# Two-layer graph attention on one core: the last three graphs' second attention is given other places in the table of steps

## The chip, the cores and the metric

The kernel runs on one core of a Trainium2 chip. TensorE (PE) multiplies, VectorE (DVE), ScalarE (ACT) and GpSimd (POOL) do the rest, and SyncE (SP) issues most DMA transfers. The metric is device time in microseconds (us), as the median of several runs. What a measurement of this kernel can tell from no change is taken to be 0.2%.

## The reference

Sixteen graphs of 1024 nodes with 256 features each go through two layers; all graphs share one adjacency matrix.

```python
h = relu(layernorm(x))
# layer 0: MLP, dense attention (no mask), MLP, attention masked by adj
out = relu(h @ mlp1_w + mlp1_b);  res = out
out = elu(gat(relu(out), None, W_fc, a_fc)) + res
out = relu(out @ mlp2_w + mlp2_b);  res = out
out = elu(gat(relu(out), adj, W_hand, a_hand)) + res
x = x + relu(out)
# layer 1: attention masked by adj
h = relu(layernorm(x))
x = x + relu(softmax(where(adj == 0, -1e9, leaky_relu(e_src + e_dst))) @ (h @ W))
```

In `gat`, h = inp @ W, the scores are leaky_relu(f1[i] + f2[j]), softmax runs over j, the weights multiply h, and the result goes through elu.

## The kernel before, in words

A graph is cut into eight tiles of 128 nodes (NT = 8); a half is four tiles, a pair is two (PAIR = 256 nodes). "a" names the first masked attention (layer 0, class Gnn0), "b" the second one (layer 1, class Gnn1). A suffix in a name of the profile is dropped: `ob` stands for the sums of the second attention of every graph.

The softmax weight of a masked attention factors. For a query row i and a node j it is max(row[i], w[j]) times the mask, with a factor d[j] that is put on the features beforehand. So a masked attention has these steps:

- `project` (L322, L324): features and the two score columns of a tile, TensorE `pa` or `pb`, copied by ScalarE to `hma` or `hmb`.
- `extremes` and `vectors` (L329 to L351): the largest score over all nodes by way of a small TensorE transpose (`extps`), then the exponentials `qwd`.
- `row` (L360 or L364): qwd's row on all partitions. Either it goes through DRAM and comes back by a DMA (`rowsa<-row_a`), or, for graph 0's and the last two graphs' steps, eight TensorE transposes write it to PSUM (`rowsps`) and ScalarE copies it in one piece (L364).
- `scale` (L368): ScalarE puts d[j] on the features of tile j, in place.
- `weight` (L373): VectorE makes 128 x 256 weights (`atta`, `attb`) for one pair of query tiles and one j. Eight buffers exist (ATT = 8), shared by a and b and by the dense attention of graph 0.
- `product` (L384): TensorE adds, for both tiles of the pair, the product with the features of tile j, into `oa` or `ob`. A matmul in float32 shows as two rows of the trace.
- `finish` (L396 to L400, L420 to L422): reciprocal on VectorE, Relu with this scale on ScalarE. For a, `combine` follows: two exponentials on ScalarE (L405, L406) and two adds on GpSimd (L408, L409); the adds are on VectorE for graph 0 alone. `update` adds to x on VectorE (L413 for a, L426 for b). `store` writes a half of x to DRAM from SP (L429).

The dense attention sorts nodes by score. GpSimd gathers rows of two tables of running sums from DRAM (`got`, L637, fine and coarse). `share` (L649 to L652, `den`) and `mean` (L659 on ScalarE, L661 on VectorE, `hp`) weigh them. `merge` transposes four `hp` for one of four feature chunks (L708, `hpT`), takes the minimum on VectorE (L710), two exponentials on ScalarE (L711, L712), and `merge_end` a maximum and sum on VectorE (L718) and an add on GpSimd to `resT` (L719). `mlp2` (L726) needs all four chunks of a half of `resT`; its result `oT` is projected to `pa`, and `natural` transposes it back (`on`, L740) to `o_nat` (L742 on ScalarE), which `combine` adds. `Norm` has `stats` (L262, L263 on VectorE), `root` (L267, L268 on GpSimd, a half at a time), `center` (L272 on VectorE, `hn`) and `turn` (L282 on TensorE, `nt`; L286 on ScalarE, `hT`).

PSUM has four buffers for matmul results (`mm`: project, products, MLPs), two for transposes (`tr`: extps, on, hpT, nt) and one for rows.

The order of the work is written by hand. `at(lo, hi, steps)` enters steps in a table at evenly spaced due times from lo on; the times are in about microseconds but are only used to sort. The sorted table is issued step by step, and each engine then runs its own instructions in exactly that order; a step waits only for data and for buffers. GpSimd's order is fixed in the same way. So a step that waits on an engine holds up all that stand behind it on that engine.

```python
    def base_of(b):
        return b * PERIOD - SHORT * (b > 0)      # PERIOD 142, SHORT 28
    ...
        for _, _, step in sorted(table, key=lambda entry: entry[:2]):
            ...
            step()
```

In the steady state a graph's second attention is done between the steps of the following graphs: its pair 0 before the next graph's first attention, its pairs 1 to 3 after that. Graph 13 (third from the end) still does so. Graph 14 does three pairs early, among the merges of graph 15, and the last pair after the first attention of graph 15. Graph 15 has nothing beside it. `dense_end` holds graph 15's share, mean and merges, which are set 10 later than for the others (`late`).

Of the kernel before, what the change touches and what calls it, by code (L numbers as in the profile page):

```python
# [31 lines left out]
def fast_path(ctx: ExitStack, tc: tile.TileContext, alarm, x, adj, w1, b1, w2, b2, w_fc, a_fc,  # L32
# [269 lines left out]
    class Masked:  # L302
# [53 lines left out]
        def row(self, sent=False):  # L356

            self.rows = work.tile([P, N], F32, tag="rows", name=f"rows{self.name}")
            if sent:
                nc.sync.dma_start(self.rows, row_d[self.which][self.b % 2].to_broadcast([P, N]))  # L360
            else:
                rows_ps = bc_psum(f"rowsps{self.name}")
                row_broadcast(rows_ps, cols(self.qwd[:, 0, :]))
                nc.scalar.copy(self.rows, rows_ps)  # L364
# [5 lines left out]
        def weight(self, q, j):  # L370

            a_t = big.tile([P, PAIR], F32, tag="att", name=f"att{self.name}_{q}_{j}", bufs=ATT)
            nc.vector.scalar_tensor_tensor(a_t, self.rows[:, q * PAIR:(q + 1) * PAIR],  # L373
                                           self.qwd[:, 1, j:j + 1],
                                           edge[:, j, q * PAIR:(q + 1) * PAIR], op0=OP.max,
                                           op1=OP.mult)
            self.att[q, j] = a_t

        def product(self, q, j):

            for t in (2 * q, 2 * q + 1):
                if j == 0:
                    self.out[t] = mm_psum(f"o{self.name}_{t}")
                nc.tensor.matmul(self.out[t][:, :F + self.ONES],  # L384
                                 lhsT=self.att[q, j][:, (t % 2) * P:(t % 2 + 1) * P],
                                 rhs=self.hm[:, j, 2:2 + F + self.ONES], start=(j == 0),
                                 stop=(j == NT - 1))

    class Gnn0(Masked):
# [13 lines left out]
        def combine(self, t, o_nat):  # L403
# [3 lines left out]
            adder = nc.vector if self.beside_gathers else nc.gpsimd  # L407
# [8 lines left out]
    class Gnn1(Masked):  # L416
# [11 lines left out]
        def store(self, h, xt, b):  # L428
            nc.sync.dma_start(out[b, h * HALF:(h + 1) * HALF, :].rearrange("(t p) f -> p t f", p=P),  # L429
                              xt[:, h * TH:(h + 1) * TH, :])  # L430
# [412 lines left out]
    def dense_end(t0, b):  # L843
        d = dense[b]
        late = 10 * last(b)
        for h in range(NH):
            lo = t0 + late + 78 + 13.4 * h
            at(lo, lo, [partial(d.share, h)])
            lo = t0 + late + 78.2 + 14 * h
            at(lo, lo + 1.5, each(d.mean, [h], range(TH)))  # L850
            merges(t0 + late + 85 + 13.2 * h, d, h)
        second_mlp(t0, b)
# [5 lines left out]
    def second_mlp(t0, b, after=0):  # L858
        d, m = dense[b], gnn0[b]
        for i, lo in enumerate((102.5, 104.8, 113, 116.5)):  # L860
            lo += t0 + 10 * last(b)
# [5 lines left out]
    def weights(m, q, lo, hi):  # L867
        at(lo, hi, each(m.weight, [q], range(NT)))

    def masked_first(t0, b):  # L870
# [10 lines left out]
        weights(m, 0, lo - 5.5, lo - 1)  # L881
        at(t0 + 10, t0 + 10, [partial(load_again, b)])
        at(t0 + 4.5, t0 + 11, each(dense[b].natural, range(NT // 2)))
        at(lo, lo + 28, each(m.product, range(NQ), range(NT)))
        for q in range(1, NQ):
            weights(m, q, lo - 5.5 + 7 * q, lo + 1 + 7 * q)
        for t in range(NT):
            end = lo + 7.2 + 7 * (t // 2) + 0.6 * (t % 2)
            at(end, end, [partial(m.finish, t)])
            at(end + 1.2, end + 1.2, [lambda t=t: m.combine(t, dense[b].o_nat)])  # L890
            at(end + 5.2, end + 5.2, [lambda t=t: m.update(t, xs[b])])
            end += 6.2 if last(b) or b == 0 else 9
            at(end, end, [partial(n.stats, t)])
        at(lo + 25, lo + 25, [partial(n.root, 0)])
        lo += 35.5 if last(b) or b == 0 else 38.5
# [5 lines left out]
    def second_norm(t0, b):  # L901
        n, m = norm2[b], gnn1[b]
        if last(b):
            n.turn_at(t0 + 46.5, 0)
            n.turn_at(t0 + 49, 1, 1.6)
            lo = t0 + 50
        elif b == 0:
            n.turn_at(t0 + 47, 0)
            n.turn_at(t0 + 50.5, 1, 1.6)
            lo = t0 + 47.2  # L910
        else:
# [5 lines left out]
        if last(b, 2):  # L917
            at(lo + 7.8, lo + 7.8, [m.vectors])
            at(lo + 8.2, lo + 8.2, [m.row])
            at(lo + 8.3, lo + 9.5, each(m.scale, range(NT)))  # L920
# [6 lines left out]
    def masked_second(parts, b):  # L927

        m = gnn1[b]
        for q, lo in enumerate(parts):  # L930
            at(lo, lo + 7, each(m.product, [q], range(NT)))
            weights(m, q, lo - 5.5, lo - 0.1)
            for u in range(2):
                t = 2 * q + u
                end = lo + 7.2 + 0.6 * u
                at(end, end, [partial(m.finish, t)])
                at(end + 1.5, end + 1.5, [lambda t=t: m.update(t, xs[b])])
            if q % 2:
                end = lo + 10
                at(end, end, [lambda h=q // 2: m.store(h, xs[b], b)])  # L940
# [79 lines left out]
    for b in range(NB):  # L1020
        base, after_base = base_of(b), base_of(b + 1)
        masked_first(base, b)
        second_norm(base, b)
        if last(b):
            parts = [base + 65 + 7 * q for q in range(NQ)]
        elif last(b, 2):
            parts = [base + 86, base + 94.5, base + 107.5, after_base + 39]
        else:
            parts = [after_base + lo for lo in (11, 46, 53, 60)]
# [21 lines left out]
    made, last = [], None  # L1051
    engine = mybir.EngineType
    with tc.manual_schedule(engines={engine.PE, engine.DVE, engine.Activation, engine.SP}):
        for _, _, step in sorted(table, key=lambda entry: entry[:2]):
# [4 lines left out]
            for ins in traced[n:]:  # L1059
                if ins.engine != engine.Pool:  # L1060
                    continue
                before = [] if last is None else [last]
                if is_scatter:
                    made.append(ins)
                else:
                    before, made, last = before + made, [], ins
# [446 lines left out]
```

## Time and profile before

| | us |
|---|---|
| median of 3 runs (2361.68 to 2363.62) | 2363.11 |
| the profiled execution, in all | 2353.15 |
| its span, first to last instruction | 2351.4 |
| TensorE busy in the span | 2271.9 |
| VectorE busy | 1620.2 |
| ScalarE busy | 1241.4 |
| GpSimd busy | 955.0 |

The prediction's sums are made against the span; what lies around it in that execution is 1.75 us. In the profile a group of instructions is named by line, engine and operation, and by the tile that it writes and those that it reads. PEclk is the share of TensorE's full clock that the throttle granted. A wait says which engine stood idle for which instruction of another engine, with the total, the number of times and the longest, in us. Idle time of an engine that doesn't set the end costs nothing.

### The profile page before, as it was taken

The numbers are of one execution on the slowest core, as the hardware profiler recorded it, in microseconds if no ns is written. First come the engines' busy times: TensorE is split into PE (matmuls) and PEld (weight loads), VectorE is DVE, ScalarE is ACT, GpSimd is POOL, SyncE is SP. The second block draws the span as 40 slices with busy tenths as digits, with TensorE's granted clock in tenths as the row PEclk, the third lists the DMA queues.
The fourth block names the chain that finished last, engine by engine and source line by source line (L and its number), as shares of the span: only waits on it lengthen the run. The fifth ranks groups of instructions, "written<-read, shape, count | busy, mean of one in ns | idle before, by whom it ended". The sixth has DMA issues, their size and how long they took to land. (4 is left out here: it accounts for less than half of the span.)

```text
span 2351.4 us, 30828 instructions
## 1 busy us (share of the span) xinstructions
PE 2271.9 (97%) x9955; PEld 1751.2 (74%) x9955; DVE 1620.2 (69%) x4499; ACT 1241.4 (53%) x2740; POOL 955.0 (41%) x1216
## 2 busy tenths in 40 slices
PE   8989999999999999999999999999999999999897
PEld 6667787777868777786876877777786877778676
DVE  6666685866858577685866767586685857758554
ACT  5345655647365554736556374564736556463442
POOL 1153435353433526444353533535344352634320
PEclk9999999999999999999999999999999999999898
DMA  4658366582646647275563645657265664637400
GB/s 175 166 160 208 72 178 163 168 199 102 196 117 171 179 158 189 90 192 145 180 180 133 176 109 177 160 169 192 105 194 118 175 179 152 186 101 199 109 1 29
DMA packets 150762, 355.81 MB, mean 151 GB/s; under 512 B 11112, under 2 KB 62648, under 8 KB 146496
## 3 DMA queue, kind: packets, MB, share of 16 engines
q1 hardware_dynamic: 103968, 189.58, 28.1%
q0 software_dynamic: 45952, 163.99, 26.3%
q8 instruction: 82, 1.34, 0.2%
q14 instruction: 88, 0.72, 0.1%
q10 hardware_dynamic: 672, 0.17, 0.0%
HBM read 227.40 MB, written 126.30 MB: 150 GB/s over the span
## 5 line engine op out<-in xcount | busy, mean ns | idle before, releaser
L384 PE MATMUL ob<-hmb,attb 128*128 128x257 f32 x2048 | 467.7, 386 | 11.8 <-DVE attb L373 11.6
L465 PE MATMUL h<-wfc_sb,resT 128*128 128x257 f32 x2048 | 465.5, 380 | 0.0
L384 PE MATMUL oa<-hma,atta 128*128 128x258 f32 x2048 | 455.5, 382 | 1.3 <-DVE atta L373 1.2
L384 PEld LDWEIGHTS ob<-hmb,attb 128*128 128x128 f32 x2048 | 388.9, 193 | 78.0 <-DVE attb L373 10.9
L384 PEld LDWEIGHTS oa<-hma,atta 128*128 128x128 f32 x2048 | 389.2, 190 | 60.2 <-issue 2.0
L465 PEld LDWEIGHTS h<-wfc_sb,resT 128*128 128x128 f32 x2048 | 379.5, 190 | 53.5 <-issue 0.7
L719 POOL TENSOR_TENSOR resT<-resT,e 128x512 f32<-128x512 f32 x128 | 163.4, 1276 | 374.3 <-DVE e L718 331.7
L408 POOL TENSOR_TENSOR posa<-posa,onat 128x256 f32<-128x256 f32 x120 | 100.5, 837 | 470.3 <-ACT posa L400 470.3
L373 DVE SCALAR_TENSOR_TENSOR atta<-rowsa,qwda,edge 128x256 f32<-128x256 f32 x512 | 267.3, 552 | 25.4 <-PE oa L384 14.3
L373 DVE SCALAR_TENSOR_TENSOR attb<-rowsb,qwdb,edge 128x256 f32<-128x256 f32 x512 | 243.6, 518 | 11.0 <-PE ob L384 8.4
L422 ACT ACTIVATE rb<-ob,recb 128x256 f32<-128x256 f32 x128 | 59.2, 476 | 341.5 <-DVE recb L420 338.5
L726 PE MATMUL m<-resT,w_sb 128*128 128x512 f32 x512 | 231.4, 598 | 4.4 <-POOL resT L719 4.4
L451 PE MATMUL m<-hT,w_sb 128*128 128x512 f32 x512 | 234.2, 596 | 0.5 <-ACT posa L400 0.5
L637 POOL DMA_INDIRECT got<-coarse,k x124 | 200.9, 1620 | 39.1 <-issue 35.1
L399 ACT ACTIVATE ea<-oa,reca 128x256 f32<-128x256 f32 x128 | 60.8, 475 | 265.3 <-DVE reca L396 265.3
L710 DVE TENSOR_SCALAR e<-hpT 128x512 f32<-128x512 f32 x128 | 88.4, 690 | 137.7 <-PE hpT L708 105.3
L726 PEld LDWEIGHTS m<-resT,w_sb 128*128 128x128 f32 x512 | 94.1, 192 | 107.0 <-issue 91.1
L451 PEld LDWEIGHTS m<-hT,w_sb 128*128 128x128 f32 x512 | 92.3, 192 | 95.3 <-issue 90.9
L637 POOL DMA_INDIRECT got<-fine,k x124 | 126.3, 1019 | 62.8 <-issue 33.4
L525 POOL DMA_INDIRECT sorted<-hnat,place x128 | 131.7, 1029 | 39.5 <-issue 18.9
L548 ACT ACTIVATE junk<-r,fs 128x1024 int8<-128x1024 f32 x124 | 142.4, 1148 | 6.5 <-POOL fs L469 5.5
L711 ACT ACTIVATE e<-e 128x512 f32<-128x512 f32 x128 | 80.7, 631 | 86.5 <-DVE e L710 86.4
(186 smaller groups left out, 3450.4 us busy)
## 6 DMA issues: line engine op xcount, KB each, us to landing
xs<-sorted SPq DMA_DIRECT2D x32, 1028.0 KB
fine<-tt SPq DMA_DIRECT2D x32, 1026.0 KB
fine<-xs SPq DMA_DIRECT2D x32, 1026.0 KB
x<-in_x_dram SPq DMA_DIRECT2D x16, 1024.0 KB
out_dram<-x SPq DMA_DIRECT2D x32, 512.0 KB
xn<-in_x_dram SPq DMA_DIRECT2D x15, 1024.0 KB
coarse<-carry SPq DMA_DIRECT2D x32, 256.5 KB
r<-row_r SPq DMA_DIRECT2D x14, 512.0 KB
```

Source lines behind the costliest of these rows:

```text
L373: nc.vector.scalar_tensor_tensor(a_t, self.rows[:, q * PAIR:(q + 1) * PAIR], self.qwd[:, 1, j:j + 1], edge[:, j, q * PAIR:(q + 1) * PAIR], ...
L384: nc.tensor.matmul(self.out[t][:, :F + self.ONES], lhsT=self.att[q, j][:, (t % 2) * P:(t % 2 + 1) * P], rhs=self.hm[:, j, 2:2 + F + self.O ...
L408: adder.tensor_add(pos, pos, o_nat[:, t, :])
L451: nc.tensor.matmul(ps, lhsT=w1_sb[:, kc, c * P:(c + 1) * P], rhs=hT[:, kc, h * HALF:(h + 1) * HALF], start=(kc == 0), stop=(kc == FC - 1))
L465: nc.tensor.matmul(ps[:, :F + 1], lhsT=self.resT[:, kc, t * P:(t + 1) * P], rhs=wfc_sb[:, kc, g, :], start=(kc == 0), stop=(kc == HC - 1))
L525: made = nc.gpsimd.indirect_dma_start(out=sorted_d[self.b % 2], out_offset=bass.IndirectOffsetOnAxis(ap=self.place[:, t:t + 1], axis=0), i ...
L548: nc.scalar.activation(junk, self.r2, AF.Sign, bias=self.fs[:, 0, t:t + 1], accum_out=self.signs[:, t:t + 1])
L637: nc.gpsimd.indirect_dma_start(out=got[u // n][:, u % n, :], out_offset=None, in_=(coarse_d if coarse else fine_d)[self.b % 2][:, :], in_o ...
L710: nc.vector.tensor_scalar_min(e, ps, 0.0)
L711: nc.scalar.activation(e, e, AF.Exp)
L719: nc.gpsimd.tensor_add(dst, dst, e)
L726: nc.tensor.matmul(ps, lhsT=w2_sb[:, kc, c * P:(c + 1) * P], rhs=self.resT[:, kc, h * HALF:(h + 1) * HALF], start=(kc == 0), stop=(kc == H ...
```

## The change

Only the places of steps, the size of a few pieces and one choice of engine change; the arithmetic is the same.

- `weight`, `product` and `store` take a first tile and a number of tiles instead of a pair or a half. Products of a part are entered in two groups, the last two j apart (`mid`).
- Graph 13: pair 0's weights are made 9.5 earlier; of pair 3, the last two j come 12.8 after the first six.
- Graph 14: parts are pairs 0 and 1, and then tiles 4, 5, 6, 7 alone. Pair 0 comes 8 earlier, pair 1 8.5 earlier, tile 4 9 earlier; tiles 5 and 6 come after graph 15's first attention, tile 7 after graph 15's second projection, its last two j behind the others. Each part is stored by itself.
- Graph 15: share, mean, merges and mlp2 come 13.4 earlier (`late` from +10 to -3.4). In both attentions the last pair is two single tiles. The adds of tiles 6 and 7 in its first attention go to VectorE as steps of their own (`add`), and norm steps move.
- Graphs 14 and 15: the four `natural` steps are spread between the steps of `vectors` and `row`. A row that comes from PSUM is copied in two pieces, 256 columns and 768; this holds for graph 0's first row too.

```diff
-                nc.scalar.copy(self.rows, rows_ps)
+                for i in (slice(0, PAIR), slice(PAIR, N)):
+                    nc.scalar.copy(self.rows[:, i], rows_ps[:, i])
...
-            adder = nc.vector if self.beside_gathers else nc.gpsimd
+            if not (last(self.b) and t >= NT - 2):
+                self.add(t, o_nat, nc.vector if self.beside_gathers else nc.gpsimd)
+
+        def add(self, t, o_nat, adder):
+            e, pos = self.out[t]
             adder.tensor_add(pos, pos, o_nat[:, t, :])
             adder.tensor_add(e, e, pos)
...
-        late = 10 * last(b)
+        late = -3.4 * last(b)
...
-            lo = t0 + late + 78.2 + 14 * h
-            at(lo, lo + 1.5, each(d.mean, [h], range(TH)))
+            lo = t0 + late + (78.2 + 14 * h if not last(b) else 80 + 12.2 * h)
+            at(lo, lo + 1.5 + 2 * last(b), each(d.mean, [h], range(TH)))
...
-            lo += t0 + 10 * last(b)
+            lo += t0 - 3.4 * last(b)
...
+        if last(b, 2):
+            for q, start in enumerate((0.5, 2, 4.2, 5.5)):
+                at(t0 + start, t0 + start, [partial(dense[b].natural, q)])
+        else:
+            at(t0 + 4.5, t0 + 11, each(dense[b].natural, range(NT // 2)))
+        pairs = [(t, 2) for t in range(0, NT, 2)]
+        if last(b):
+            pairs[-1:] = [(NT - 2, 1), (NT - 1, 1)]
...
+            if last(b) and t >= NT - 2:
+                at(end + 2.6, end + 2.6, [lambda t=t: m.add(t, dense[b].o_nat, nc.vector)])
+                end -= 2
...
-        at(lo + 25, lo + 25, [partial(n.root, 0)])
-        lo += 35.5 if last(b) or b == 0 else 38.5
+        at(lo + 25 - 3.4 * last(b), lo + 25 - 3.4 * last(b), [partial(n.root, 0)])
+        lo += 33.1 if last(b) else 35.5 if b == 0 else 38.5
...
-            at(lo + 7.8, lo + 7.8, [m.vectors])
-            at(lo + 8.2, lo + 8.2, [m.row])
-            at(lo + 8.3, lo + 9.5, each(m.scale, range(NT)))
+            at(lo + 7.1, lo + 7.1, [m.vectors])
+            at(lo + 9.2, lo + 9.2, [m.row])
+            at(lo + 9.3, lo + (10.5 if last(b) else 17), each(m.scale, range(NT)))
...
+        for lo, t, n, *apart in parts:
+            mid = apart[0] if apart else lo + 2.6 * n
+            at(lo, lo + 2.6 * n, each(m.product, [t], [n], range(NT - 2)))
+            at(mid, mid + 0.9 * n, each(m.product, [t], [n], range(NT - 2, NT)))
+            early = 5.5
+            if t == 0 and last(b, 3):
+                early = 2.6 if last(b, 2) else 15
+            weights(m, t, n, lo - early, lo - early + 5.4)
...
+            if last(b, 2):
+                at(end + 2.8, end + 2.8, [lambda t=t, n=n: m.store(t, n, xs[b], b)])
...
         if last(b):
-            parts = [base + 65 + 7 * q for q in range(NQ)]
+            parts = [(base + 65 + 3.5 * t, t, 2) for t in pairs[:-1]]
+            parts += [(base + 65 + 3.5 * t, t, 1) for t in (NT - 2, NT - 1)]
         elif last(b, 2):
-            parts = [base + 86, base + 94.5, base + 107.5, after_base + 39]
+            parts = [(base + 78, 0, 2), (base + 86, 2, 2), (base + 98.5, 4, 1),
+                     (after_base + 39, 5, 1), (after_base + 42.5, 6, 1),
+                     (after_base + 57.2, 7, 1, after_base + 59.3)]
         else:
-            parts = [after_base + lo for lo in (11, 46, 53, 60)]
+            parts = [(after_base + lo, t, 2) for lo, t in zip((11, 46, 53, 60), pairs)]
+            if last(b, 3):
+                parts[-1] = (after_base + 60.4, NT - 2, 2, after_base + 73.2)
```

## The prediction

> **What bounds the kernel now.** I read the page first.
>
> ```profile
> span 2351.4 us, 30828 instructions
> PE 2271.9 (97%) x9955; PEld 1751.2 (74%) x9955; DVE 1620.2 (69%) x4499; ACT 1241.4 (53%) x2740; POOL 955.0 (41%) x1216
> PEclk9999999999999999999999999999999999999898
> ```
>
> TensorE is busy 97% of the span at the full granted clock, until the last slices. The new program has the same 9128 TensorE instructions as the old in number, and the built order of every engine is the old one up to about 2105 us of this trace (only one ScalarE copy of graph 0 is cut in two). So only the last 245 us can move: the end of graph 13, and graphs 14 and 15. The table by stage says where they lose time (after the window: its length, PE, PEld, DVE, ACT and POOL busy, clock, DMA share, GB/s):
>
> ```profile
> 2110.00:2185.00 75.00, 71.36 (x333) 60.91 (x331) 57.29 (x149) 30.19 (x77) 35.87 (x36) 0.98 0.76 207
> 2185.00:2245.00 60.00, 48.60 (x176) 33.20 (x176) 32.58 (x75) 26.66 (x47) 12.21 (x12) 0.86 0.30 71
> 2245.00:2302.00 57.00, 49.99 (x229) 41.72 (x229) 35.16 (x93) 25.16 (x61) 15.40 (x21) 0.94 0.01 5
> 2302.00:2352.00 50.00, 39.11 (x169) 32.87 (x167) 20.51 (x61) 11.56 (x29) 0.00 (x0) 0.88 0.09 29
> ```
>
> Two losses stand here: idle TensorE (11.4 us in the second row) and a clock of 0.86 to 0.94. The waits of TensorE from 2100 us on name the first:
>
> ```profile
> PE ob L384 <- DVE attb L373: 5.5, 3, 2.1
> PE on L740 <- ACT onat L742: 2.9, 3, 1.2
> PE nt L282 <- ACT rb L422: 2.6, 1, 2.6
> PE hpT L708 <- DVE hp L661: 2.6, 3, 1.5
> PE m L726 <- POOL resT L719: 2.4, 2, 1.3
> PE rowspsb L238 <- ACT qwdb L347: 2.1, 2, 1.2
> ```
>
> With the smaller rows TensorE's gaps from 2110 us on add up to 25 us. The clock I followed in short windows. It is set in steps of 3.41 us, and a step runs at half rate when TensorE was little busy in the step before it:
>
> ```profile
> 2182.76:2186.17 3.41, 1.65 (x8) 0.96 (x6) 1.06 (x7) 0.85 (x4) 2.80 (x4) 1.00 1.06 224
> 2186.17:2189.58 3.41, 1.51 (x10) 1.28 (x11) 1.40 (x5) 2.63 (x7) 0.57 (x2) 1.00 1.06 226
> 2254.43:2257.84 3.41, 1.48 (x11) 1.14 (x11) 3.12 (x8) 3.41 (x9) 0.00 (x0) 1.00 0.01 2
> 2309.05:2312.46 3.41, 1.49 (x10) 1.09 (x10) 1.95 (x13) 1.38 (x5) 0.00 (x0) 1.00 0.02 5
> 2258.00:2259.00 1.00, 1.00 (x3) 0.78 (x3) 0.00 (x0) 1.00 (x3) 0.00 (x0) 0.50 0.00 0
> ```
>
> The steps after the second, third and fourth rows (busy 1.48 to 1.51 us) ran at 0.50; the one after the first (1.65 us) at full rate. Each half step full of work loses 1.7 us. After 2110 us about 13 us go this way.
>
> Here **a rule of the Trainium skill** differs: "TensorE: Matmul & The Clock Gate", section "Why this matters for your kernels", asks for no idle gaps over about 3 us. The longest gap here is 2.6 us, so by the rule no half step would arise and closing gaps would win the gaps alone. The trace shows half steps after several shorter gaps that add up to 1.9 us. I go by the trace. By the rule the clock's terms below drop out (1.7 at oa, 2.85 at ob 15, some 4.6 in the merges), and the sum would be 5.5 us instead of 14.6.
>
> **The change, stage by stage.** At full clock a matmul row of L384 takes 217 ns, an instruction (two such rows) 0.434 us, a tile's eight 3.47 us. Before: ob of graph 14 starts at 2189.2, pa of 15 at 2243.5, oa at 2257.6, pb at 2301.2, ob of 15 at 2313.6, the last matmul ends at 2344.4.
>
> *Up to ob of graph 14.* Transposes of o_nat now fill the gaps beside extpsa (L740's 2.9 us), and the first eight attb of graph 13 are made while VectorE idles 4.9 us before exta; their rows landed at 2086. But oa of graph 14 needs atta from rowsa, which lands at 2121.7 whatever TensorE does: it can start at about 2122.9 instead of 2124.0, gain 1. Next rstd waits for GpSimd's queue. Four products of ob 13 (1.74 us) now fill the wait before rowspsb; the gap after rowspsb (1.7 us) stays. New waits: recb of graph 13 stands behind the four den, and den needs the gathers' landing, at 2187 (the gathers' traffic falls at 2197 for the second half; the second store of graph 13, now later, frees about 1.6 us). On ScalarE the rows copy stands behind rb of that recb, and all eight scales of hmb behind it. Splitting the copy (1.01 us) lets attb start 0.6 us earlier, but hmb's first scale follows both pieces, so it brings nothing. ob 14 starts at 2188.9: gain 0.3 (between -1.5 and +3; nearest the low row, as the chain den, recb, rb, rows, hmb adds up to the 2.8 us that the filled wait and the earlier start win). Its half step I leave in (even chance).
>
> *ob 14 with the merges of graph 15, the largest term.* Before: 54.4 us. share, mean and merges move 13.4 us ahead in the table, and ob tile 5 goes out (3.47 us). Work: 40 x 0.434 + 8 transposed groups x 0.44 + 16 rows of m2 x 0.86 = 34.6 us. VectorE must deliver, from den to the last hp of the second half, 16 attb x 0.40 + 8 hp x 0.67 + 8 merge steps x 0.60 + den, recb and updates 3.5 = 20 us, plus about 2 us behind ScalarE's part and 2.5 us that a GpSimd add costs it. The last follows from these rows: beside GpSimd's adds the same instruction takes double.
>
> ```profile
> 2287.17 0.94 DVE L373 SCALAR_TENSOR_TENSOR attb<-rowsb,qwdb,edge 128x256 f32<-128x256 f32 x1
> 2288.37 0.47 DVE L373 SCALAR_TENSOR_TENSOR attb<-rowsb,qwdb,edge 128x256 f32<-128x256 f32 x1
> ```
>
> So the last hp comes at about 2212, where TensorE would need it at 2208: a wait of 3.8 instead of today's 6.1 (2.1+1.4+1.5+0.6+0.5). With 0.7+0.7 for two transposes, 1.9 before the last quarter of m2 (merge 0.7, ScalarE 0.63+0.72, merge 0.68, GpSimd 1.27 after its transpose, less 2.6 of m2 in between; today 2.35) and 3.2 for half steps: 34.6+3.8+1.4+1.9+3.2 = 45.0. Gain 54.4-3.5-45.0 = 6 (3 to 10).
>
> *pa to oa of graph 15.* From pa's end to oa 6.9 us now. After: on 0 fills the first gap, extps ends at +1.0, on 1 at +1.75, rowsps at +3.0, on 2 and 3 at +3.9; ScalarE's rows (0.4+0.8), onat (0.6) and first scale (0.5) end at +5.1. Gain 1.8, and no step stays under 1.6 us: 1.7 more. 3.5 (2 to 4).
>
> *oa 15 to pb 15.* Tiles 6 and 7 become single, their adds go to VectorE, root 0 moves ahead, ob 14's tiles 5 and 6 lie around the transposes. In VectorE's order the last atta of tile 7 stands behind four attb that wait for buffers of att (8) and four hn; it comes 0.7 to 2.2 us late. Behind it stand nine attb, three updates, three stats and two adds (6 us) ahead of tile 7's recb; then ScalarE 1.9, add, update and stats 1.4, GpSimd 1.4, hn 0.4 to 1.4. So pb follows oa's end by 12.5 us instead of 14.1, and oa ends 1.7+0.7 later than its work: about +0.5 loss (-3 to +3). The 128-wide instruction isn't in this trace; between nothing and the 0.40 of 256 columns I take 0.27, half the columns at the same start-up.
>
> *pb to ob 15.* Gaps 0.8, 0.9 and 1.6 and two half steps (2.85 us). Eight products of tile 7 (3.47 us) fill two of the gaps; after, 0.76+0.3+2.17+1.09+1.6 = 6.0 against 4.75 before plus 3.47 moved in: gain 2.2, and 2.85 of clock. Against it: x's last update of graph 14 stands ahead of the fourth attb and waits for rb, which stands behind eight scales on ScalarE (3.3 us): TensorE stops 1.5. Net 3.6 (2 to 5).
>
> *The end.* From the last matmul 7.0 us: reciprocal, Relu, update 1.2, a 512 KB store. Its packets take 2.4 us; 128 KB a quarter of it: gain 1.7 (1 to 2). SP's queue gets 11 stores for these two graphs instead of 4: behind graph 14's third stands x's load for 15, needed 30 us later, behind the others nothing. On GpSimd's queue only root 0 of graph 15 passes four adds, and a memset of hmb the last gather.
>
> Sum: 0.3+6+3.5-0.5+3.6+1.7 = 14.6; span 2351.4 to 2336.8. The profiled execution took 2353.15 in all; the median of the runs is 2363.11, 10 us above it. I carry the difference over: 2348.5.
>
> **Rivals.**
> 1. *All bubbles close*: VectorE keeps up, no half step but one. Left are some 8 us of gaps out of 25 and 2 of clock out of 13; the gain is 25 to 28, time 2337. For it: VectorE is 54% busy from 2185 to 2245. Against: the waits named are for VectorE.
> 2. *The bubbles only move*: a VectorE wait takes the place of each one closed in the merges and in oa's end; left are pa-oa 3.5 and the store 1.7 less 1 to 5: 2358 to 2363.
> 3. *Slower*: VectorE's queue bounds graph 15's first attention. From atta of tile 7 to hn of tile 7 stand about 50 instructions; if waits for att buffers and GpSimd's adds cost each 0.5 us on average, 25 us, it outweighs the rest: 2370. It decides from 0.4 us each. Against: only the adds of tiles 4 and 5 (3 us) run beside them.
> That the change doesn't do what it says is out: the built order shows it.
>
> **How the numbers follow.** Forecast 0.60, rival 1 0.18, rival 2 0.16, rival 3 0.06. Range 2337 to 2358. Bound of measurement 0.2% (4.7 us): faster 0.85 (forecast, rival 1, part of 2), same 0.10, slower 0.05. The forecast's own range is 2340 to 2356.
>
> **What would show it.** Until 2105 us the same trace. ob 14 at about 2189; pa 15 near 2234; TensorE's wait for hp under 4.5 us; waits for onat near 0; no half step at oa's start nor at ob 15's; a TensorE wait for atta near the end of oa 15, a gap of about 3 us before nt's second half; a stop of 1.5 us in ob 15's first pair; 5.3 us after the last matmul. Wrong if pa 15 isn't ahead of 2240, or the half steps stay in number.

## The result, and the profile after

The changed kernel takes 2356.33 us (median of 7 runs, 2351.53 to 2359.75), the kernel before beside it 2363.62 (7 runs, 2361.68 to 2366.51): a ratio of 0.9963, 95% interval 0.9951 to 0.9974. It is faster by some 7 to 9 us, where 14.6 were forecast. A second comparison (`after_again` below) gives 0.9961 (0.9948 to 0.9973): about 9 us. So the sign stands, and the size is half of the forecast or a little more. The median lies inside the whole range of 2337 to 2358, and 0.3 us above the range of the forecast case (2340 to 2356).

The page of the changed kernel, the lines that answer to those shown of before:

```profile
span 2357.9 us, 30868 instructions
PE 2268.6 (96%) x9955; PEld 1747.4 (74%) x9955; DVE 1625.7 (69%) x4535; ACT 1241.3 (53%) x2744; POOL 951.4 (40%) x1212
PEclk9999999999999999999999999999999999999999
```

The span of this execution is 6.5 us longer than the one of before (2351.4), though the kernel is faster. The order of instructions is the old one up to graph 14's `pa`, yet `pa` of graph 14 begins at 2116.5 us here and at 2103.1 before; in the profiles of the edits below it lies anywhere between 2096.5 and 2109.6. So the two profiles can't be compared by their spans. From `pa` of graph 14 to the end of the span they can: 248.3 us before, 241.4 after, 6.9 less.

The same windows as in the prediction, cut at the same distances from the same products (columns as there):

```profile
2123.42:2203.66 80.24, 71.31 (x329) 59.72 (x328) 54.53 (x142) 29.26 (x75) 36.52 (x38) 0.98 0.77 194
2203.66:2256.02 52.36, 43.36 (x165) 29.34 (x164) 31.79 (x76) 26.74 (x49) 11.72 (x11) 0.93 0.34 83
2256.02:2309.76 53.74, 47.09 (x231) 39.88 (x231) 37.98 (x116) 25.34 (x62) 12.43 (x17) 1.00 0.01 3
2309.76:2357.90 48.14, 39.31 (x183) 33.27 (x182) 23.51 (x78) 12.03 (x31) 0.00 (x0) 0.97 0.09 30
```

The last three stages are 60.0, 57.0 and 50.0 us before and 52.4, 53.7 and 48.1 now, and their clock rose from 0.86, 0.94 and 0.88 to 0.93, 1.00 and 0.97. The first stage went the other way, from 75.0 to 80.2. TensorE's waits from 2116 us on, longest groups first:

```profile
PE oa L385 <- DVE atta L375: 5.5, 3, 2.4
PE ob L385 <- DVE attb L375: 4.7, 2, 3.4
PE nt L282 <- DVE hn L272: 4.1, 2, 2.9
PE ob L385 <- ACT hmb L369: 3.7, 3, 2.1
PE hpT L713 <- DVE hp L666: 2.7, 4, 0.9
PE m L731 <- POOL resT L724: 2.2, 2, 1.1
...
PE on L745 <- ACT onat L747: 0.5, 2, 0.3
```

The wait for onat is nearly gone (2.9 before). That for hp is unchanged under this name (2.6), but of the 6.1 us of waits that the forecast counted there, the 2.1 for attb ahead of the merges are gone. New in the list are waits for atta, for hn and for the scaled hmb. TensorE's gaps above 0.15 us, from `pa` of graph 14 on, still add up to 26.7 us, 25 before, although 3.5 us of products were moved into them; 3.4 of the 26.7 are one wait behind a table that landed late in this execution (below). What fell is the clock's loss: ten steps at half rate (half steps) between 2105 us and the last product before, three now. Two of them with the steps ahead of them (windows as above):

```profile
2204.37:2207.78 3.41, 1.38 (x11) 1.03 (x9) 1.96 (x10) 1.94 (x6) 0.00 (x0) 1.00 1.06 208
2207.78:2211.19 3.41, 3.37 (x8) 2.72 (x9) 2.01 (x5) 3.41 (x8) 0.00 (x0) 0.50 1.06 209
2228.26:2231.68 3.42, 1.66 (x8) 0.87 (x8) 3.29 (x5) 1.23 (x2) 1.39 (x1) 1.00 0.00 0
2231.68:2235.09 3.41, 2.81 (x7) 1.94 (x7) 3.41 (x12) 2.07 (x4) 0.32 (x1) 0.50 0.00 0
```

1.38 and 1.66 us of TensorE work, and the next step at half rate: the wait for hmb at the start of ob 14, and the waits for hp.

Stage by stage, from the starts of the named tiles' products in the two traces (us; a gain is positive; 3.5 us of products moved from the second row to the fifth):

| stage | before | after | gain | forecast |
|---|---|---|---|---|
| pa to ob of graph 14 | 86.1 | 91.3 | -5.2 | 0.3 |
| ob of 14 to pa of 15, less the work moved | 54.4 | 46.7 | 4.2 | 6 |
| pa to oa of 15 | 14.1 | 12.3 | 1.8 | 1.8, and 1.7 of clock |
| oa to pb of 15 | 43.6 | 42.1 | 1.5, of which 1.7 clock | -0.5 |
| pb of 15 to the last product, with the work moved in | 43.2 | 42.3 | 4.4 | 3.6 |
| last product to the end | 7.1 | 6.7 | 0.3 | 1.7 |
| sum | 248.3 | 241.4 | 6.9 | 14.6 |

### The profile page after: what moved, and what is told of

The parts are those of the page before. It is cut to its first block, busy times and chain, and to the rows that moved or that the text cites. A ratio compares the mean times of both kernels' runs of the same rounds, so it can differ in the third digit from the quotient of the medians.

```text
span 2357.9 us, 30868 instructions
## 1 busy us (share of the span) xinstructions
PE 2268.6 (96%) x9955; PEld 1747.4 (74%) x9955; DVE 1625.7 (69%) x4535; ACT 1241.3 (53%) x2744; POOL 951.4 (40%) x1212
## 5 line engine op out<-in xcount | busy, mean ns | idle before, releaser
L375 DVE SCALAR_TENSOR_TENSOR atta<-rowsa,qwda,edge 128x256 f32<-128x256 f32 (+1 forms) x520 | 268.4, 545 | 27.6 <-PE oa L385 12.8
L375 DVE SCALAR_TENSOR_TENSOR attb<-rowsb,qwdb,edge 128x256 f32<-128x256 f32 (+1 forms) x536 | 247.9, 503 | 8.9 <-PE ob L385 5.5
L642 POOL DMA_INDIRECT got<-fine,k x124 | 125.7, 1013 | 74.4 <-DMA fine<-xs 41.9
```

The source lines that it names most:

```text
L375: nc.vector.scalar_tensor_tensor(a_t[:, :n * P], self.rows[:, i], self.qwd[:, 1, j:j + 1], edge[:, j, i], op0=OP.max, op1=OP.mult)
L642: nc.gpsimd.indirect_dma_start(out=got[u // n][:, u % n, :], out_offset=None, in_=(coarse_d if coarse else fine_d)[self.b % 2][:, :], in_o ...
```

## The experiments

Each kernel was compared with the kernel before on the same chip. Before takes 2351.2 us (median) beside the first four, 2350.0 beside the next four, 2356.2 beside the next three and 2350.7 beside the last; so ratios are compared, and 0.001 is 2.35 us. Theory at the start: the change works as forecast in graph 15's merges and attentions, and the 5.2 us lost ahead of `ob` of graph 14 are no work of it. Rivals: graph 13's part causes that loss; the bubbles only move.

**Graph 13's part undone** (`g13_back`)

```diff
-                early = 2.6 if last(b, 2) else 15
+                early = 2.6 if last(b, 2) else 5.5
...
-            if last(b, 3):
-                parts[-1] = (after_base + 60.4, NT - 2, 2, after_base + 73.2)
```

> The changed kernel with graph 13's part undone: its first attb again 5.5 us ahead of their products instead of 15, its last pair of ob again in one piece. In the changed kernel's profile the stage from pa to ob of graph 14 takes 91.3 us where it took 86.1 before (forecast 85.8). Theory: that loss is no work of the change; the table fine landed 3.5 us later in that one execution, GpSimd's gathers waited for it, and all behind them. Then this kernel's stage lies anywhere from 86 to 91 and its time is the changed kernel's or up to 2.8 us above it (four products no longer fill the wait before rowspsb, 1.7, and the start of oa, 1). Rival: graph 13's part causes the loss; then the stage is back at 86 in the profile and the time is 4 to 5 us below the changed kernel's, some 12 us below before.

Ratio 0.9948 (0.9935 to 0.9960); pa to ob of graph 14 takes 87.2 us. Neither theory is met in full: the stage isn't at 91, but without any edit it isn't at 91 in the other profiles either (below). Against three other profiles on this chip with graph 13's part in (87.7, 88.6 and 88.7) it is shorter by 0.4 to 1.5 us, and the ratio is lower by 0.0012 to 0.0015, within the intervals. So graph 13's part brings nothing that these runs show, and may cost 1 us (by the profiles) to 3 (by the ratios). In its profile the first row operation of graph 14 on VectorE after exta follows 0.3 us sooner: with the change two attb of graph 13 stand between exta and topa (at 7.8 to 8.7 us after pa), and not all eight in the idle time ahead of exta, as I had it.

**Merges and ob of graph 14 back** (`merges_back`)

```diff
-        late = -3.4 * last(b)
+        late = 10 * last(b)
...
-            parts = [(base + 78, 0, 2), (base + 86, 2, 2), (base + 98.5, 4, 1),
-                     (after_base + 39, 5, 1), (after_base + 42.5, 6, 1),
-                     (after_base + 57.2, 7, 1, after_base + 59.3)]
+            parts = [(base + 86, 0, 2), (base + 94.5, 2, 2), (base + 107.5, 4, 2),
+                     (after_base + 39, 6, 2)]
```

(and the places of mean and mlp2 as before)

> The changed kernel with the largest term undone: share, mean, merges and m2 of graph 15 again 13.4 us later in the table, ob of graph 14 again in four pairs at their old places (so its tile 7 no longer fills the waits before ob of graph 15). Theory (the forecast's terms): 6 us from the merges and 3.6 from pb to ob are lost again, the time goes up by 7 to 10 us against the changed kernel, to about before or above. Second theory, by the stages of the changed profile: ob to pa of graph 15 gives 4.1 net of the 3.5 of work that moved, and what follows pb 1: up by 4 to 6. Rival (the bubbles only move): up by 2 at most.

0.9982 (0.9975 to 0.9989), 0.0019 to 0.0021 above the changed kernel: 4.5 to 5 us, give or take some 3 by the two intervals. The second theory fits best; of the forecast's 7 to 10 only the low end is not excluded. In its profile ob of 14 to pa of 15 takes 52.5 us, and pb of 15 to the last product 41.1, without tile 7's 3.5 us; with them it is 42.3. So tile 7's products found 2.3 us of waits to lie in (forecast 2.2), and the rest of the 4.5 to 5 us, about 2.4, is what the merges bring here, with the same uncertainty.

**Graph 15's first attention in pairs** (`oa15_pairs`)

```diff
-        if last(b):
-            pairs[-1:] = [(NT - 2, 1), (NT - 1, 1)]
...
-            n.turn_at(t0 + 42.4, 0, 8.2)
-            n.turn_at(t0 + 47.5, 1, 2.2)
+            n.turn_at(t0 + 46.5, 0)
+            n.turn_at(t0 + 49, 1, 1.6)
```

(and adds, stats and root as before)

> The changed kernel with graph 15's first attention as before: tiles 6 and 7 as a pair, their adds on GpSimd, root and hn at their old places. Forecast: the single tiles lose 0.5 us (-3 to +3), so this gains about 0.5. By the stages of the changed profile (oa to pb of graph 15: 43.6 before, 42.1 after) they win 1.5: this stage is 43.6 again and the time 1.5 us above the changed kernel's. Rival: VectorE's queue (the adds of tiles 6 and 7 on it) costs more than it brings, and the pair is 2 to 3 us faster.

0.9970 (0.9959 to 0.9982), 0.0007 to 0.001 above the changed kernel, about 2 us, which these intervals can't tell from none; the stage takes 43.1 instead of 42.1, what follows 43.8 instead of 42.3, two half steps between them. By the profiles the single tiles win 1 to 2.5 us; VectorE's queue did not become the bound.

**The end as before** (`end_by_half`)

```diff
-            parts = [(base + 65 + 3.5 * t, t, 2) for t in pairs[:-1]]
-            parts += [(base + 65 + 3.5 * t, t, 1) for t in (NT - 2, NT - 1)]
+            parts = [(base + 65 + 3.5 * t, t, 2) for t in pairs]
...
-            if last(b, 2):
+            if last(b, 2) and not last(b):
                 at(end + 2.8, end + 2.8, [lambda t=t, n=n: m.store(t, n, xs[b], b)])
```

> The changed kernel with graph 15's end as before: the last two tiles of ob as a pair, two stores of 512 KB instead of stores by pair and tile. Forecast: from the last matmul to the end of the span 7.0 us instead of 5.3, time 1.7 us above the changed kernel's. By the changed kernel's profile (6.74 us after the last matmul where it was 7.06 before) the size of the store hardly sets the end: 0.3 us, time the same. Rival: many small stores cost on the queue, and the end by half is faster by 0.5 or more.

0.9960 (0.9947 to 0.9973): as with the change. From the last product to the end of the span 6.74 us, the very number of the changed kernel. Over all profiles of this study the end takes 5.6 to 7.4 us with a last store of 128 KB (eleven profiles, middle one 6.9) and 6.7 to 7.1 with 512 KB (three). No effect of the store's size is seen.

**The changed kernel once more** (`after_again`), no edit

> The changed kernel once more, without an edit, on the chip and beside the runs of the edits that follow. If the table fine is late only now and then (it was late in graphs 5, 7, 11, 13 and 15 of the changed kernel's first profile and in none of four edits run on another chip), the first gather of graph 15 goes 14.2 us after the table's last issue and the stage from pa to ob of graph 14 takes 87 to 89 us, not 91.3. If the change makes it late, it is 91 again.

0.9961 (0.9948 to 0.9973). No table is late in this profile after graph 1, and pa to ob of graph 14 takes 89.1 us (a half step among them). So most of the loss in the first profile is GpSimd's wait for the table of graph 15: behind it VectorE is late, and TensorE waits 3.4 us for attb where `after_again` has no wait. GpSimd's wait for it, first in the changed kernel's first profile (2150 to 2190 us):

```profile
POOL got L642 <- DMA fine<-xs: 3.7, 1, 3.7
```

and in the profile of the kernel before with the edit `before_fill` (2137 to 2175 us), where these stages are before's own:

```profile
POOL got L641 <- DMA fine<-xs: 2.3, 1, 2.3
```

The kernel before has a late table too in this run, and takes 89.7 us from pa to ob of graph 14. Before's first profile has no such wait there. So the late landing is not the change's. Without it the changed order takes 87.5 to 89.3 us in seven further profiles (with graph 13's part in), against 86.1 for before's order without the late table and 89.7 with it. The lengths also vary by a half step that comes or goes, so the gaps of TensorE in this stage tell more. With the wait behind the late table left out (3.4 and 1.9 us) they add up to 4.8 and 4.5 us with before's order, and to 5.5 to 6.7 in the first profile and the seven with the change: the new order has some 1 to 2 us more of waits here.

**linea ahead of the second onat** (`line_first`)

```diff
-            for q, start in enumerate((0.5, 2, 4.2, 5.5)):
+            for q, start in enumerate((0.5, 2 if last(b) else 3.5, 4.2, 5.5)):
```

> The changed kernel with one transpose group of o_nat of graph 14 moved behind the sending of its row (place 3.5 instead of 2), so that ScalarE copies linea before the second onat. Theory: in the changed kernel linea's copy stands behind that onat, 0.74 us later than before; rowsa lands 1.1 us later, and atta, the adds on GpSimd, rstd and hn all shift by it, which is most of the 2.15 us that TensorE now waits ahead of nt before pb of graph 14. Then here GpSimd's first add comes 1.1 us earlier after pa, the wait before nt is about 1.0, and the time 1.1 us below the changed kernel's. Rival (the forecast's view: rowsa lands when it lands, rstd waits for GpSimd's gathers): no change in the wait and in the time.

0.9966 (0.9954 to 0.9977), no better than the change. linea is copied 0.5 us sooner (9.8 us after pa of graph 14, 10.3 with the change), but rowsa's load is issued at 15.0 instead of 15.1, as the row's own write now takes 4.9 us to land instead of 4.6, and the first atta comes at 19.9 (20.1). GpSimd's first add and the wait before nt (2.2 us) stay. The theory fell in this run; the landings outweighed the earlier copy, as the rival said. Over all profiles the first atta comes at 18.6 to 19.6 in the six without graph 13's part and at 19.6 to 20.1 in the eight with it, so some tenths of the delay seem to be that part's. Before's profile, where atta came at 18.6, has the shortest landing of rowsa of all (3.8 us from its issue; 4.4 to 5.0 in every other profile, before's order included).

**Two groups of m2 together** (`m2_pairs`)

```diff
+        def mlp2_both(self, h):
+            ps = [mm_psum(f"m2_{self.b}_{h}_{c}") for c in range(FC)]
+            for first in range(0, HC, 2):
+                for c in range(FC):
+                    for kc in (first, first + 1):
+                        nc.tensor.matmul(ps[c], lhsT=w2_sb[:, kc, c * P:(c + 1) * P],
...
-            at(lo, lo, [partial(d.mlp2, i // FC, i % FC)])
+            if not last(b) or i < FC:
+                at(lo, lo, [partial(d.mlp2, i // FC, i % FC)])
+            elif i == FC:
+                at(lo, lo, [partial(d.mlp2_both, 1)])
```

> The changed kernel with the last two groups of m2 of graph 15 taken together: kc 0 and 1 of both output halves, then kc 2 and 3 of both, so that 1.7 us of products fill the waits of 1.08 and 1.11 us for resT. By the waits alone: ob to pa of graph 15 is 1.7 us shorter. By the clock as the traces show it (a step of 3.41 us with 1.60 us of TensorE work or less halves the next): the half step 43 us after ob of graph 14, seen in two of four profiles, also goes, 1.7 us more where it was; so 1.7 to 3.4 us below the changed kernel. Rival: GpSimd's last add to resT comes later than all this, and the wait only moves: 0.

0.9957 (0.9944 to 0.9970), 1 us below the change, which these intervals can't tell from none. The profile is plain: the waits of 1.08 and 1.11 us for resT became one of 0.74, the half step 43 us after ob of graph 14 is absent, and the stage takes 46.0 us with the two half steps at 22 us still in it (49.4 with the change on the same chip).

**Extra products before the transposes** (`fill_hpT`)

```diff
             for u in range(TH):
+                if last(self.b) and (h, c) == (1, 0):
+                    nc.tensor.matmul(ps[:, u * P:(u + 1) * P], lhsT=ident, rhs=ident,
+                                     start=True, stop=True)
                 nc.tensor.transpose(ps[:, u * P:(u + 1) * P], self.hps[h, u][:, lo:lo + P], ident)
```

> The changed kernel with four extra products of 128 columns (about 0.27 us each), one ahead of each transpose of the first merge of the second half of graph 15, where TensorE waits 0.9, 0.55 and 0.93 us for hp; what they write is overwritten by the transposes. They bring nothing but TensorE work in the waits. By the clock as the traces show it: the step there has 1.33 us of work, with the extra ones about 2.1 to 2.4, so the half steps after it (one in the changed kernel's profile, two in two others, at 21 to 24 us after ob of graph 14) go: 1.7 to 3.1 us faster. By the rule that only idle gaps over about 3 us cost clock: no half step depends on it, time the same or up to 0.4 us slower.

The rule meant here and in `before_fill` is the one that the prediction names. In the profile the edit does what the traces' clock says. The step of 3.41 us with the waits for hp, and the one after it, first in the profile of `m2_pairs` (no extra products there), then in that of `fill_hpT` (length, PE, PEld, DVE, ACT and POOL busy, clock, DMA share, GB/s):

```profile
2205.05:2208.47 3.42, 1.48 (x6) 0.54 (x4) 2.78 (x5) 2.49 (x4) 0.40 (x1) 1.00 0.00 0
2208.47:2211.88 3.41, 2.66 (x8) 2.10 (x9) 3.41 (x8) 0.84 (x2) 1.71 (x1) 0.50 0.00 0
```

```profile
2213.65:2217.06 3.41, 2.26 (x14) 1.60 (x14) 3.28 (x5) 1.35 (x2) 1.26 (x1) 1.00 0.00 0
2217.06:2220.48 3.42, 2.82 (x11) 1.65 (x10) 3.42 (x12) 1.96 (x4) 0.45 (x1) 1.00 0.00 0
```

With 2.26 us of work the next step runs at the full clock, with 1.48 at half. But the time is the change's, 0.9960 (0.9946 to 0.9975): other half steps stand in this profile (at 2125, 2180 and 2234 us), and an effect of 2 us is not to be seen in one comparison of this width. The next run makes it larger.

**The same in the kernel before, where three half steps follow each other** (`before_fill`)

```diff
             for u in range(TH):
+                if self.b == NB - 1 and (h, c) == (1, 0):
+                    for _ in range((8, 8, 3, 3)[u]):
+                        nc.tensor.matmul(ps[:, u * P:(u + 1) * P], lhsT=ident, rhs=ident,
+                                         start=True, stop=True)
...
                     self.out[t] = mm_psum(f"o{self.name}_{t}")
+                    if self.which == "b" and self.b == NB - 2 and t == 4:
+                        for _ in range(6):
+                            nc.tensor.matmul(self.out[t][:, :F], lhsT=ident,
+                                             rhs=self.hm[:, 0, 2:2 + F], start=True, stop=True)
```

> The kernel before with extra products that only keep TensorE at work in graph 15's merges, all overwritten: six of 256 columns (0.22 us each) ahead of ob tile 4 of graph 14, where TensorE waits 2.14 us, and 8, 8, 3 and 3 of 128 columns (0.11 each) ahead of the four transposes of the first merge of the second half, where it waits 1.4, 1.5, 0.6 and 0.5. In before's profile the step of 3.41 us ahead of them has 1.18 us of work and three half steps follow (10.2 us, at 20.9 us after ob of graph 14). By the clock as the traces show it: with the extra work no step there is under 1.6 us, the three half steps go, 10.2 us at half rate become some 6.5, ob to pa of graph 15 is 50.5 instead of 54.4 and the time 3 to 4 us below before. By the rule that only gaps over about 3 us cost clock: the half steps stay, 0 to 0.5 us slower. The stages up to ob of graph 14 are before's own, a second profile of them: 86.1 from pa to ob if that is what before takes on this chip; 87 to 88 if the changed kernel has lost nothing there; rowsa's load lands 3.8 us after its issue if the 4.5 to 5.0 seen with the change are the change's, else later.

0.9985 (0.9976 to 0.9994): the kernel before becomes 3.5 us faster by 28 products whose results are thrown away. (This is 0.15%, less than the 0.2% taken as the bound; with 22 runs against 27 the interval still excludes no change.) ob of 14 to pa of 15 takes 50.2 us (54.4 before, 50.5 expected), and the four steps that answer to the one of 1.18 us and the three at half rate are full of work at the full clock (windows):

```profile
2207.97:2211.38 3.41, 3.41 (x19) 3.06 (x19) 3.17 (x7) 2.19 (x4) 1.24 (x2) 1.00 0.00 0
2211.38:2214.80 3.42, 3.42 (x31) 3.34 (x29) 1.31 (x3) 2.38 (x5) 1.18 (x1) 1.00 0.00 0
2214.80:2218.21 3.41, 3.41 (x28) 3.17 (x27) 3.41 (x8) 0.91 (x2) 0.00 (x0) 1.00 0.00 0
2218.21:2221.62 3.41, 3.41 (x20) 2.99 (x19) 3.41 (x7) 0.00 (x0) 1.44 (x1) 1.00 0.72 207
```

No gap of before in this stage is over 2.14 us. So gaps well under 3 us cost clock here, and the trace's reading is borne out by a time, not by a profile alone.

**Three edits together** (`best`): graph 13's part undone, m2 in pairs, the four extra products

> The changed kernel with three edits together: graph 13's part undone, the last two groups of m2 taken together, and the four extra products ahead of the first merge of the second half. By the traces' clock: no half step is left in the merges, ob to pa of graph 15 takes about 44 us (46.4 to 49.4 with the change), pa to ob of graph 14 about 87 (87.7 to 89.1); the time is 3 to 5 us below the changed kernel's, a ratio to before of 0.994 to 0.995. By the gaps alone the extra products bring nothing: 2 us below the changed kernel's.

0.9955 (0.9939 to 0.9971), 1.5 us below the change by ratio; 3 to 5 were expected and 2 by the gaps alone. The stage takes 44.3 us, as expected, but not in the way expected: two half steps stand in it, at its start and 24 us later, where none was to be left. What the stage won is not seen in the time at this width. Open.

**Tile 4 of graph 14 moved too** (`tile4`)

```diff
-            parts = [(base + 78, 0, 2), (base + 86, 2, 2), (base + 98.5, 4, 1),
-                     (after_base + 39, 5, 1), (after_base + 42.5, 6, 1),
+            parts = [(base + 78, 0, 2), (base + 86, 2, 2), (after_base + 38.8, 4, 1),
+                     (after_base + 40.8, 5, 1), (after_base + 43.4, 6, 1),
```

> The same as the kernel with three edits, and ob tile 4 of graph 14 moved as well, from the merges to the end of graph 15's first attention, where TensorE waits 2.9 us for hn ahead of nt's second half. If VectorE bounds the merges (as the waits for hp say), its eight attb of tile 4 leave with the products: ob to pa of graph 15 is 3 us shorter, and the moved 3.5 us of products lie in the wait for hn: 2 to 3 us below the three edits alone. Rival: the eight attb come ahead of tile 7's atta and hn in VectorE's queue and hn is later by what they take (2 us), and tile 4's products find no wait: 0 to 1.5 us slower than the three edits alone.

0.9939 (0.9922 to 0.9956), 3.8 us below the three edits alone by ratio; the intervals overlap. ob of 14 to pa of 15 is 39.3 us instead of 44.3; oa to pb of 15 is 44.7 instead of 41.9: of the 3.5 us of products, 0.7 found a wait, and VectorE's eight attb leave the merges, where it was late. That is 2.2 us in the two stages, within the 2 to 3 expected, though less of it than expected comes from filled waits; a further 1.7 is a half step after pb of 15 that `best` had and this one hasn't. The filled wait stood just ahead of it, but other profiles with that wait have no half step either, so this part may be chance.

**x's update of graph 14 behind the first two pairs** (`update_late`)

```diff
+                later = 4 * bool(apart and last(b, 2))
-                at(end + 1.5 + 0.6 * u, end + 1.5 + 0.6 * u, [lambda t=t + u: m.update(t, xs[b])])
+                at(end + 1.5 + 0.6 * u + later, end + 1.5 + 0.6 * u + later,
+                   [lambda t=t + u: m.update(t, xs[b])])
```

> The kernel with tile 4 moved, and x's last update of graph 14 (with its store) 4 us later in the table, behind the attb of ob's first two pairs of graph 15. The forecast names it as what stops TensorE in ob's first pair of graph 15: the update stands ahead of the fourth attb and waits for rb, which stands behind eight scales on ScalarE. With the change TensorE stops 1.22 to 1.24 us there, 6.7 us after rowspsb begins, in all profiles. Theory: that stop is gone, from rowspsb of graph 15 to the last product 30.8 us instead of 32.07, and the time 1.2 us below the kernel with tile 4 moved (ratio to before 0.9934). Rival: the next attb wait for something else (buffers of att, the scales of hmb), and the stop only moves: 32.07 again.

0.9924 (0.9910 to 0.9937). TensorE's waits from rowspsb of graph 15 to the end, in the profile of `tile4` (2298 to 2340 us):

```profile
PE ob L385 <- DVE attb L375: 1.2, 1, 1.2
PE ob L385 <- ACT hmb L369: 0.2, 1, 0.2
```

and in that of `update_late` (2289 to 2325 us):

```profile
PE ob L385 <- ACT hmb L369: 0.2, 1, 0.2
```

The stop is gone, and from rowspsb to the last product it takes 30.6 us instead of 32.1. That the update ahead of the fourth attb was the cause is shown. The ratio fell by 0.0015, some 3.5 us, where 1.2 were expected; by the intervals it can't be told from that. This version beats both kernels: 18 us below before, some 9 below the change.

## Why the prediction was right, and where its sum failed

*Right.* The forecast case came true in sign, and its larger part in kind: of the 14.6 us some 9.2 were to come from the clock, 3.8 from shorter waits and 1.7 from the end. The clock's loss fell, from ten half steps to between one and six in the six profiles of the change whose merges are its own. The part of the waits mostly failed: TensorE's gaps from pa of graph 14 on add up to 24.2 to 24.9 us in the four of these profiles that have graph 13's part and no late table, 25.3 before, and to 21.6 in `g13_back`. These terms held:

- pa to oa of graph 15: 14.06 us in both profiles of before's order, 12.31 or 12.32 in all twelve of the changed one; 1.75 us won, 1.8 forecast, and the half step at oa's start is gone in all twelve.
- oa to pb of 15: 43.6 less the 1.7 of that half step, against 42.1: 0.2 lost, 0.5 forecast. The late atta (1.8 us) and the wait of 2.9 us before nt's second half are there as named.
- pb to the last product: 4.4 won, 3.6 forecast. The stop of 1.5 us by x's update measured 1.22, and its cause was shown by moving it. That the term as a whole is 0.8 better than forecast is luck as far as the sum goes: it hides part of what is missing elsewhere.
- waits in the merges: 2.7 for hp (3.8 forecast), 2.2 for resT (1.9 forecast, though the parts that the prediction gives for it add up to 1.4).
- "I go by the trace": `before_fill` decides for the trace, against the rule of 3 us. The Trainium skill's page "TensorE: Matmul & The Clock Gate" also has a section, "A second HAM failure mode: psum-queue depth-cycling", that speaks of frequent short idle times making the clock swing; that is the passage which fits this kernel, where the list in "Why this matters for your kernels" doesn't.

*Wrong,* the steps that made 14.6 out of about 8 to 9:

- *The end, 1.7 us.* The step took the last store's time as if it grew with its packets' 2.4 us. The term measured 0.3 in the two profiles and 0.0 in the comparison by one edit. The Trainium skill's page "DMA: Bandwidth & Descriptors", section "Anatomy of one DMA — SWDGE (gpsimd) path", has most of a small transfer's time as a fixed part, and its fit would give an estimate of 0.9 us for 384 KB less. That section is on transfers issued by GpSimd, and this store is issued by SP; the runs show less still.
- *The merges, 6 us.* They measured 4.2 in the first profile, 1.5 to 4.5 in the others whose merges are the change's own, 2.4 in `merges_back`. Two things were left out of the sum of 45.0. The last hmb scale of graph 14 now stands behind the first merge's exps on ScalarE, as the scales are spread to 17 in the table, and ob's products of the last j wait 1.5 us for it (0.5 in `g13_back` and `best`). ScalarE's timeline in the changed kernel's first profile (start, length, what, idle time before it and its end):

```profile
2216.39 0.63 ACT L716 ACTIVATE e<-e 128x512 f32<-128x512 f32 x1 [2.77 <-DVE e L715]
2217.05 0.72 ACT L717 ACTIVATE e<-e,neg 128x512 f32<-128x512 f32 x1
2217.68 0.49 ACT L369 ACTIVATE hmb<-hmb,qwdb 128x257 f32<-128x257 f32 x1
```

  The exps wait 2.8 us for VectorE's e, and the scale, which needs nothing from them, stands behind. The other thing is the half steps, for which 3.2 us stood in the sum: there are one to three of them there (some 1.7 to 4.8 us), by where the waits fall in the steps of 3.41 us. With the same gaps of 7.5 us the stage takes 46.4 us in `line_first`, with one half step, and 49.4 in `after_again`, with three.
- *Up to ob of graph 14, 0.3.* Without the late table the gaps say a loss of 1 to 2 us. rowsa does not land at 18.6 us after pa "whatever TensorE does": that was one short landing. The gaps beside extpsa were closed, and oa now waits up to 2.7 us for atta and starts only 0.2 to 0.7 us sooner than in before's profile (1 forecast). The wait before rowspsb was filled, and a wait of 1.2 to 2.2 us for hn opened ahead of nt (0.3 before). Where the four products are back in their old place (`g13_back`, `best`, `tile4`, `update_late`) it is still 1.3, so moving them explains at most 0.9 of it; the rest was not tried. This is the rival "the bubbles only move" in two places.
- *The first profile's 5.2 us* there were not forecast, and 3.4 of them are not the change's: GpSimd's queue stood 3.7 us for a table that landed late.
- *The signs.* "Wrong if pa 15 isn't ahead of 2240": it begins at 2254.6 in the first profile, 138.0 us after pa of graph 14, where 136.9 were asked for and 140.4 stood before. In the five other profiles with the change's merges it begins at 2234.6 to 2239.7, or 133.7 to 138.5 after pa of 14. So this sign is met in part only. The other one, fewer half steps, is met in all.

Not shown: how the missing 5 to 6 us divide to the last microsecond, since a stage varies by up to 3 us from one profile to the next.

## What to carry to other kernels

Where a schedule is written by hand, ask of each product that is moved into a wait which wait it had covered; the chain behind that wait, not TensorE, may set the stage. Look at TensorE's work in each step of the clock and not only at the longest gap: here a few short waits in one step cost up to 1.7 us more in the next, and work put into them, even useless work, won it back. Compare two profiles only from the point where the orders part, and take a second profile of the old order before a loss is put down to a change.

## What the runs showed that I had not expected

- The same busy time ends differently by the clock at which it was spent. Over all fourteen profiles, a step at half rate that was busy for up to 2.7 us (2.31 in before, 2.66 in `m2_pairs`) was followed by another half step, and one busy for more than 3.0 us never was; between these both occur. A step at the full rate with 2.31 us of work was always followed by a full one. So it looks as if work is counted, and not time busy. For a step at the full rate the limit is not sharp in these traces: with up to 1.48 us of work the next step was always at half rate, above 1.92 never, and between them both occur (1.65 in before was followed by a full step, 1.66 in the changed kernel at 2228.3 us by a half one).
- The landing of the same table differs from chip to chip: no wait of GpSimd for it after graph 1 in the nine profiles taken beside a before of 2350 to 2351 us; in one to three graphs of each profile, by up to 2.4 us, beside a before of 2356.2; and in the changed kernel's first profile in six graphs, by up to 3.8 us, beside a before of 2363.6. In before's own first profile it is two graphs, by up to 1.6 us. The rank of the first three is the same; that the landings make the 12 us between them wasn't tried.
